# A two-layer transformer kernel: block inputs also sent in by feature, bfloat16 transposes by DMA, biases folded into weights

## The chip, the cores and the metric

The kernel runs on one core of a Trainium2 chip. A core has a matrix engine (TensorE, PE in the profile, with its weight loads as PEld), a vector engine (VectorE, DVE), a scalar engine (ScalarE, ACT), a general engine (GpSimd, POOL) and a queue engine (SyncE, SP). SBUF is the on-chip memory with 128 partitions; matmuls write to PSUM. DMAs are issued from the queues of SP, ACT and POOL. The metric is the device time of the program in microseconds; here it is the median over runs, 1665.76 us.

## The reference: what is computed

The input x has 2 sequences of 2048 tokens with 512 features; a context has 2 x 128 tokens with 512 features. Two layers, each with cross attention and a feed-forward part, are added to x one after the other:

```python
x = x + _L0_xattn_ref(_layernorm(x), ctx, ctx, mask_pad, Wq, Wk, Wv, Wo, ln_g, ln_b)
x = x + _L0_ffn_ref(_layernorm(x), clip_x, clip_down, w_gate, w_up, w_down)
x = x + _L1_xattn_ref(_layernorm(x), ctx, ctx, mask, Wq, bq, Wk, bk, Wv, bv, Wo, bo)
x = x + _L1_ffn_ref(_layernorm(x), Wg, bg, We, be)
```

- Layer 0's attention: a second layer norm with gain and offset (`ln_g`, `ln_b`) on x and on the context, 16 heads of 64 with rotary positions, scores through `30 * tanh(s / 30)`, causal mask and padding mask, softmax, values, output projection.
- Layer 0's feed-forward part: 512 to 1408 and back, `silu(gate) * up`, where activations and weights are rounded to 8-bit steps (weights with a step for each row, activations with one step for the whole tensor).
- Layer 1's attention: 16 heads of 32, biases on all projections, masked scores set to 1e-9, softmax over all 128 keys.
- Layer 1's feed-forward part: a gate of 512 classes; the class with the largest probability, modulo 8, picks one of 8 experts:

```python
probs = softmax(x @ Wg + bg)
idx = argmax(probs)
h = relu(x @ We[e] + be[e])      # e = idx % 8
out = h * probs[idx]
```

## The kernel before

x stays in SBUF as 32 tiles of 128 tokens x 512 features (`xs`, inside `xw`). Matmuls contract over partitions, so whatever is multiplied by a weight must be turned first, with features on the partitions. The kernel turns tiles on TensorE against an identity matrix and copies the result from PSUM to SBUF.

**Layer 0's attention** goes over 16 blocks of 256 tokens (`blocks`, two tiles each), four head groups to a block: 64 units `u`, where `k, g = divmod(u, 4)`. In a unit, `scores(u)`, `queries(u + 2, 0)`, `mixed(u - 1)`, `queries(u + 2, 1)` and `projected(u - 2, t)` follow each other. Before a block can be queried it is normed: `normed(k)` (statistics of each tile, the power -1/2 on POOL), `centered(k)` (subtract the mean, multiply by rstd, on DVE), `turned(k, c0)` (four TensorE transposes, then ACT applies gain and offset on the way from PSUM to `xnT`). `normed` and `centered` of block k + 2 run in the unit g = 2 of block k; `turned(k + 1, ...)` in the units g = 0 and 1.

Between these units the weights of layer 0's feed-forward part are made: at g = 0 and g = 3 one of 26 tiles is quantised (`quantised`, to bfloat16 `wb`) on DVE and the next is loaded; one unit later its `turn()` transposes it on TensorE into `wgT`, `wuT` (4 transposes a tile, 22 tiles) or `wdT` (11 transposes a tile, 4 tiles).

In this stage the order of the instructions of PE, DVE and ACT is the order of the code (`manual_schedule`). POOL's and SP's order is made by the framework's planner, by the time at which it reckons each instruction ready. Every queue runs in its order: an instruction that waits holds those behind it.

**Start.** Wk, the first x tiles, Wv, Wq, more x tiles and Wo are loaded in this order on SP's queue; the weights of keys and values lie in the places of the last 23 x tiles (`homes`), whose loads follow when these are used up. The context is normed, `keys(g)` computed, and in between block 0 is normed; then come values, the first queries, and block 1.

**Layer 0's feed-forward part.** `quantised_x(n)` rounds a tile to int8 and widens it to bfloat16 `xq`; `turned_x(n)` turns it (4 transposes) into `xqT`, a block of 512 tokens. For each of 8 blocks and 11 chunks of 128 hidden features, gate and up are each 4 matmuls; the product `h` goes to DRAM. `turned_x` of the next block's four tiles stands in chunks 3, 5, 7 and 9. In this stage only PE keeps the code's order. Then the down projection reads `h` back.

**Layer 1** goes over the 32 tiles, one iteration `n` each, with several tiles in flight; here PE, DVE, ACT and POOL keep the code's order. POOL adds the output bias (`projected`, L902), makes rstd (L92) and spreads the reciprocal sums (`summed`, L864). `turned2(n)` turns the normed tile, `logits(n)` multiplies it by `wgate`; a first matmul (L927) adds the bias, from `beparts` (the biases in three bfloat16 parts) picked by `sel`. `gated(n)` finds the expert. The finished tile is written to `x_dram`. `we`, the expert weights, are loaded in iteration 0. Tokens are then sorted by expert, and `expert(j)` gathers 128 tokens of one expert, turns them (`turned_x2`), adds the bias (L1120) and multiplies by the expert's weights (L1122): 39 times, two of them within the loop and the rest in the tail.

Of the kernel before, what the change touches and what calls it, by code (L numbers as in the profile page):

```python
# [13 lines left out]
I32 = mybir.dt.int32  # L14
# [29 lines left out]
NJB = NT - NJA + NE - 1  # L44
NOWHERE = float(2**20)
# [13 lines left out]
def two_layers(ctx: ExitStack, tc: tile.TileContext, a, out):  # L59
# [15 lines left out]
    nc.vector.memset(minus_half, -0.5)  # L75

# [65 lines left out]
    with ExitStack() as l0:  # L142
# [41 lines left out]
        for n in order[:NB0]:  # L184
            load(xs[n], x_in[n])
        for c in range(ND):
            wv.append([])
            for f in range(E0 // D):
                w = xs[homes[8 + 2 * c + f]]
                load(w, a["L0_xattn_Wv"][c * P : (c + 1) * P, f * D : (f + 1) * D])  # L190
                wv[c].append(w)
# [13 lines left out]
        tables_in(0)  # L205
        load(wo, a["L0_xattn_Wo"].rearrange("(c p) f -> p c f", p=P))
# [66 lines left out]
        def gate_up_in(name, i):  # L273
            w = wtmp.tile([P, D], F32, name="w_in", tag="w_in")
            load(w, a[name][i * P : (i + 1) * P, :])
            return w

        def gate_up(w, dst, scales, i):
            wb = quantised(w, scales[:, i : i + 1])

            def turn():
                pt = psm.tile([P, ND, P], BF16, name="ptb", tag="m")
                for c in range(ND):
                    nc.tensor.transpose(pt[:, c, :], wb[:, c * P : (c + 1) * P], identb)
                nc.scalar.copy(dst[:, :, i * P : (i + 1) * P], pt)

            return turn
# [6 lines left out]
        def down(w, j):  # L294
            wb = quantised(w, sd[:, j : j + 1])

            def turn():
                for i in range(0, NI, 4):
                    n = min(4, NI - i)
                    pt = psm.tile([P, 4, P], BF16, name="ptb", tag="m")  # L300
                    for c in range(n):
                        nc.tensor.transpose(pt[:, c, :], wb[:, (i + c) * P : (i + c + 1) * P], identb)
                    nc.scalar.copy(wdT[:, i : i + n, j * P : (j + 1) * P], pt[:, :n, :])

            return turn
# [9 lines left out]
        norms, xns, xnTs, ropes, qs, prs, atts, pws = {}, {}, {}, {}, {}, {}, {}, {}  # L315
# [3 lines left out]
        def normed(k):  # L319


            for t, n in enumerate(tiles[k]):
                mv = variance(xs[n])
                ve = small.tile([P, 1], F32, name="ve")
                nc.vector.tensor_scalar(ve, mv[:, 1:2], 1.0 + EPS, EPS * EPS, ALU.mult, ALU.add)
                rr = small.tile([P, 1], F32, name="rr")
                nc.gpsimd.tensor_tensor(rr, ve, minus_half, ALU.pow)
                norms[k, t] = mv, rr

        def centered(k):  # L330
            xns[k] = []
            for t, n in enumerate(tiles[k]):
                mv, rr = norms[k, t]
                xn = mid.tile([P, D], F32, name="xn")
                center(xn, xs[n], mv[:, 0:1], rr)
                xns[k].append(xn)

        def turned(k, c0):

            if c0 == 0:  # L340
                xnTs[k] = mid.tile([P, ND, B0], F32, name="xnT")
            pt = psm.tile([P, 2, B0], F32, name="pt", tag="m")
            for c in range(2):
                for t, xn in enumerate(xns[k]):
                    nc.tensor.transpose(pt[:, c, t * P : (t + 1) * P], xn[:, (c0 + c) * P : (c0 + c + 1) * P], ident)  # L345
            for c in range(2):
                nc.scalar.activation(  # L347
                    xnTs[k][:, c0 + c, :], pt[:, c, :], AF.Identity,
                    bias=lnb[:, c0 + c : c0 + c + 1], scale=lng[:, c0 + c : c0 + c + 1],
# [106 lines left out]
        with tc.manual_schedule(engines={E.PE, E.DVE, E.Activation}):  # L456
            context()
            for g in range(NG):
# [3 lines left out]
                if g == 2:  # L462
                    centered(0)
            nc.vector.tensor_scalar(pad, padu, -1e30, None, ALU.mult)
            for c in range(0, ND, 2):
                turned(0, c)
# [12 lines left out]
            for u in range(nu + 2):  # L479
# [11 lines left out]
                if u > 1:  # L491
                    for t in range(0 if u + 2 < nu or u >= nu else 1, NB0):
                        projected(u - 2, t)
                if g < 2 and k + 1 < nblk:
                    turned(k + 1, 2 * g)
# [8 lines left out]
                if g == 2:  # L504
                    if k > 0:
                        largest(k - 1, 1)
                    if k + 2 < nblk:
                        normed(k + 2)
                        centered(k + 2)
# [38 lines left out]
    beparts = w1.tile([P, D], BF16, name="beparts")  # L548
    sel = w1.tile([P, NE + 1, P], BF16, name="sel")
# [50 lines left out]
    with ExitStack() as up:  # L600
# [6 lines left out]
        cxs = [kv.tile([P, D], F32, name=f"cx{b}") for b in range(B)]  # L607
# [3 lines left out]
        for b in range(B):  # L611
            nc.scalar.dma_start(out=cxs[b], in_=a["ctx_1024"][b])
# [10 lines left out]
        for b in range(B):  # L623
            pt = transposed(psm, cxs[b])
            nc.scalar.copy(ctxT[:, :, b * T : (b + 1) * T], pt)
# [42 lines left out]
        def turned_x(n):  # L668
            blk, t = divmod(n, NBF)
            if t == 0:  # L670
                xqTs[blk] = work.tile([P, ND, BF], BF16, name="xqT", bufs=2)
            pt = psm.tile([P, ND, P], BF16, name="ptx", tag="m")
# [8 lines left out]

        nc.vector.memset(beparts, 0.0)
        nc.vector.memset(ones1, 1.0)
        nc.vector.tensor_scalar(bq, bq, 1.0 / math.sqrt(DH1), None, ALU.mult)
        bparts = kv.tile([NE + 1, 3, D], BF16, name="bparts")
        brest = kv.tile([NE + 1, D], F32, name="brest")
        load(brest[:NE, :], a["L1_ffn_be"])
        load(brest[NE:, :], a["L1_ffn_bg"].rearrange("(o d) -> o d", o=1))
        for k in range(3):
            nc.vector.tensor_copy(bparts[:, k, :], brest)  # L690
            nc.vector.tensor_tensor(brest, brest, bparts[:, k, :], ALU.subtract)
        be_dram = dram.tile([3, NE + 1, D], BF16, name="be_dram")
        nc.sync.dma_start(out=be_dram.rearrange("k e d -> e k d"), in_=bparts)
        for k in range(3):
            load(beparts[16 * k : 16 * k + NE + 1, :], be_dram[k])
        rowi = kv.tile([P, 1], I32, name="rowi")
        nc.gpsimd.iota(rowi, pattern=[[0, 1]], base=0, channel_multiplier=1)
        nc.vector.tensor_scalar(rowi, rowi, 15, None, ALU.bitwise_and)
        rowf = kv.tile([P, 1], F32, name="rowf")
        nc.vector.tensor_copy(rowf, rowi)  # L700
        ei_ = kv.tile([P, NE + 1], I32, name="ei_")
        nc.gpsimd.iota(ei_, pattern=[[1, NE + 1]], base=0, channel_multiplier=0)
        nc.vector.tensor_scalar(sel, ei_.unsqueeze(2).to_broadcast([P, NE + 1, P]), rowf, None, ALU.is_equal)
# [215 lines left out]
    def turned2(n):  # L919
        pt = transposed(psm, xn2[n])  # L920
        xn2T[n] = mid.tile([P, ND, P], F32, name="xnT1", bufs=1)
        nc.scalar.copy(xn2T[n], pt)

    def logits(n):

        pl = pls[n] = psm.tile([P, D], F32, name="pl", tag="m")
        nc.tensor.matmul(pl, sel[:, NE, :], beparts, start=True, stop=False)  # L927
        for c in range(ND):
            nc.tensor.matmul(pl, xn2T[n][:, c, :], wgate[:, c, :], start=False, stop=(c == ND - 1))  # L929
# [176 lines left out]
    def turned_x2(j):  # L1106
        if j < NJ:
            pt = transposed(psm, part(6 + j % 3, [D]))
            ring[j] = part(9 + j % 3, [ND, P])
            nc.scalar.copy(ring[j], pt)  # L1110

    def expert(j):
# [6 lines left out]

        nc.tensor.matmul(pz, sel[:, bass.ds(e, 1), :], beparts, start=True, stop=False)  # L1120
        for c in range(ND):
            nc.tensor.matmul(pz, ring[j][:, c, :], we[:, bass.ds(e, 1), c, :], start=False, stop=(c == ND - 1))  # L1122
# [40 lines left out]
    for n in range(NT):  # L1163
# [29 lines left out]
        if n == 0:  # L1193
# [6 lines left out]
            for e in range(NE):  # L1200
                load(we[:, e], a["L1_ffn_We"][e].rearrange("(c p) f -> p c f", p=P))
        if not ahead:
# [78 lines left out]
```

## Time and profile before

| | |
|---|---|
| median of 3 runs | 1665.76 us (1664.41 to 1665.9) |
| time of the profiled execution | 1666.03 us |
| its span, first to last instruction | 1664.3 us |
| mean granted TensorE clock | 0.998 of full speed |

Busy time by stage (us, from the span's start; counts left out):

| stage | window | PE | DVE | ACT | POOL | DMA share |
|---|---|---|---|---|---|---|
| start | 0 to 62 | 51.60 of 62 | 23.00 | 12.55 | 15.38 | 0.87 |
| layer 0's units | 62 to 275 | 212.59 of 213 | 145.19 | 60.40 | 49.10 | 0.05 |
| layer 0's units | 275 to 560 | 284.02 of 285 | 198.30 | 81.49 | 59.20 | 0.06 |
| layer 0's end | 560 to 690 | 126.43 of 130 | 83.35 | 37.45 | 22.97 | 0.08 |
| to the feed-forward part | 690 to 738 | 44.90 of 48 | 42.69 | 18.89 | 2.46 | 0.52 |
| gate, up, down | 738 to 930 | 189.22 of 192 | 153.17 | 99.41 | 36.93 | 0.62 |
| layer 1's tiles | 1060 to 1450 | 388.45 of 390 | 338.55 | 249.16 | 77.05 | 0.06 |
| experts, tail | 1515 to 1664 | 137.55 of 149 | 50.70 | 38.94 | 67.09 | 0.32 |

A timeline line gives the start, the duration, the engine, the line of the code, the operation, output<-input, shapes, and how many like instructions are merged (x8). A group line gives busy time and the mean of one. Matmuls are pipelined, so the durations of neighbours overlap and a group's mean is longer than the step from one to the next. A DMA issue line ends with the time from the issue to the landing, where the trace shows it.

### The profile page before, as it was taken

The numbers are of one execution on the slowest core, as the hardware profiler recorded it, in microseconds if no ns is written. First come the engines' busy times: TensorE is split into PE (matmuls) and PEld (weight loads), VectorE is DVE, ScalarE is ACT, GpSimd is POOL, SyncE is SP. The second block draws the span as 40 slices with busy tenths as digits, with TensorE's granted clock in tenths as the row PEclk, the third lists the DMA queues.
The fourth block names the chain that finished last, engine by engine and source line by source line (L and its number), as shares of the span: only waits on it lengthen the run. The fifth ranks groups of instructions, "written<-read, shape, count | busy, mean of one in ns | idle before, by whom it ended". The sixth has DMA issues, their size and how long they took to land. (4 is left out here: it accounts for less than half of the span.)

```text
span 1664.3 us, 27098 instructions
## 1 busy us (share of the span) xinstructions
PE 1625.2 (98%) x10277; PEld 977.3 (59%) x10277; DVE 1176.4 (71%) x2294; ACT 709.4 (43%) x1601; POOL 390.8 (23%) x464
## 2 busy tenths in 40 slices
PE   7999999999999999999999999999999999999997
PEld 5666666666666555544444566676767666654553
DVE  3466667776667765699976678888888889875222
ACT  1223222222233222255445576666666666652222
POOL 2322222222222221100006632121211111224453
PEclk9999999999999999999999999999999999999999
DMA  9300000000000000455458750000000000113331
GB/s 331 132 15 18 20 14 20 14 20 14 20 14 8 35 18 1 141 146 158 146 155 282 248 202 15 20 21 14 20 14 20 14 21 14 46 46 103 124 118 62
DMA packets 89454, 118.24 MB, mean 71 GB/s; under 512 B 10732, under 2 KB 58146, under 8 KB 89325
## 3 DMA queue, kind: packets, MB, share of 16 engines
q1 hardware_dynamic: 80076, 96.63, 17.3%
q0 software_dynamic: 6240, 18.70, 3.5%
q8 instruction: 82, 1.34, 0.3%
q10 hardware_dynamic: 3008, 1.19, 0.3%
q14 instruction: 48, 0.39, 0.1%
HBM read 76.55 MB, written 41.77 MB: 71 GB/s over the span
## 5 line engine op out<-in xcount | busy, mean ns | idle before, releaser
L362 PE MATMUL pq<-xnT,wq 128*128 128x256 f32 x1024 | 254.4, 391 | 0.0
L420 PE MATMUL pw<-wo,att 128*128 128x512 f32 x512 | 230.8, 593 | 0.0
L362 PEld LDWEIGHTS pq<-xnT,wq 128*128 128x128 f32 x1024 | 184.4, 189 | 67.1 <-issue 38.7
L855 ACT ACTIVATE s<-s,mx 128x128 f32<-128x128 f32 x512 | 176.7, 387 | 18.0 <-DVE mx L846 18.0
L388 ACT ACTIVATE pr<-sc 128x1024 f32<-128x1024 f32 x64 | 65.9, 1030 | 237.0 <-PE sc L383 236.2
L420 PEld LDWEIGHTS pw<-wo,att 128*128 128x128 f32 x512 | 96.9, 190 | 96.4 <-issue 89.9
L410 DVE RECIPROCAL rd<-sc 128x256 f32<-128x256 f32 x64 | 112.5, 1758 | 51.3 <-PE sc L404 51.3
L372 POOL TENSOR_TENSOR q<-rt,rt 128x256 f32<-128x256 f32 x64 | 46.5, 727 | 422.4 <-DVE rt L371 422.4
L1122 PE MATMUL pz<-we,x 128*128 x312 | 140.3, 592 | 0.0
L367 DVE TENSOR_TENSOR rt<-pq,rope_cos 128x256 f32<-128x256 f32 x64 | 27.2, 425 | 141.2 <-PE pq L362 139.9
L347 ACT ACTIVATE xnT<-pt,lnb,lng 128x256 f32<-128x256 f32 x64 | 32.7, 561 | 216.2 <-PE pt L345 216.2
L813 PE MATMUL pq<-xT,wq 128*128 128x256 f32 x512 | 124.1, 385 | 0.0
L905 PE MATMUL pw<-wo,oT 128*128 128x512 f32 x256 | 115.5, 594 | 1.6 <-DVE oT L897 1.6
L929 PE MATMUL pl<-wgate,xnT 128*128 128x512 f32 x256 | 115.1, 592 | 0.0
L813 PEld LDWEIGHTS pq<-xT,wq 128*128 128x128 f32 x512 | 94.8, 190 | 28.1 <-issue 13.6
L1126 DVE TENSOR_TENSOR x<-x,x 128x512 f32<-128x512 f32 x39 | 27.0, 693 | 97.3 <-ACT x L1125 97.3
L841 DVE SCALAR_TENSOR_TENSOR s<-sc,keep 128x1024 f32<-128x1024 f32 x64 | 78.0, 1219 | 23.8 <-PE sc L833 23.8
L83 DVE BATCH_NORM_STATS2 st<-x 128x6 f32<-128x512 f32 x130 | 89.6, 689 | 6.0 <-DMA x<-in_ctx 3.7
L1122 PEld LDWEIGHTS pz<-we,x 128*128 128x128 f32 x312 | 58.9, 190 | 58.5 <-issue 56.8
L711 PE MATMUL pg<-xqT,wgT 128*128 128x512 bf16 x352 | 90.3, 379 | 0.7 <-ACT xqT L675 0.7
L711 PE MATMUL pu<-xqT,wuT 128*128 128x512 bf16 x352 | 90.3, 379 | 0.0
L716 ACT ACTIVATE gate<-pg,gsc 128x512 f32<-128x512 f32 x88 | 60.5, 687 | 68.9 <-PE pg L711 67.9
(229 smaller groups left out, 2888.9 us busy)
## 6 DMA issues: line engine op xcount, KB each, us to landing
h_dram<-h SPq DMA_DIRECT2D x88, 256.0 KB, 2.1
hq<-h_dram SPq DMA_DIRECT2D x31, 704.0 KB, 5.8
x_dram<-x SPq DMA_DIRECT2D x32, 258.0 KB, 3.0
x<-in_x SPq DMA_DIRECT2D x32, 256.0 KB, 5.7
we<-in_L_ffn_We SPq DMA_DIRECT2D x8, 1024.0 KB, 11.7
w_in<-in_L_ffn_w_gate SPq DMA_DIRECT2D x11, 256.0 KB, 2.6
w_down<-in_L_ffn_w_down SPq DMA_DIRECT2D x4, 704.0 KB, 4.1
w_in<-in_L_ffn_w_up SPq DMA_DIRECT2D x11, 256.0 KB, 2.6
```

Of the source, the lines that this page charges most:

```text
L83: nc.vector.bn_stats(out=st, in_=x)
L362: nc.tensor.matmul(pq, wqs[c // 2][:, c % 2, par, g * P : (g + 1) * P], xnTs[k][:, c, :], start=(c == 0), stop=(c == ND - 1))
L388: nc.scalar.activation(pr, sc[:, :, :B0], AF.Tanh, scale=1.0 / (math.sqrt(DH0) * GROK))
L410: nc.vector.reciprocal(rd, sc[:, 0, B0:])
L420: nc.tensor.matmul(pw, atts[u][:, f, t * P : (t + 1) * P], wo[:, 2 * g + f, :], start=(g == 0 and f == 0), stop=(g == NG - 1 and f == 1),)
L711: nc.tensor.matmul(dst, w[:, c, i * P : (i + 1) * P], xqTs[blk][:, c, :], start=(c == 0), stop=(c == ND - 1),)
L813: nc.tensor.matmul(pq, wq1[:, c, f * P : (f + 1) * P], xTs[blk][:, c, :], start=(c == 0), stop=(c == ND - 1))
L841: nc.vector.scalar_tensor_tensor(s, sc[:, 2 * half : 2 * half + 2].rearrange("p r c k -> p (r c) k"), -MASKED, keeps[n].unsqueeze(1).to_br ...
L855: nc.scalar.activation(s[:, h, :], s[:, h, :], AF.Exp, bias=mx[:, h : h + 1], **accum)
L905: nc.tensor.matmul(pw, os_[n][:, c, :], wo1[:, c, :], start=(c == 0), stop=(c == ND - 1))
L929: nc.tensor.matmul(pl, xn2T[n][:, c, :], wgate[:, c, :], start=False, stop=(c == ND - 1))
L1122: nc.tensor.matmul(pz, ring[j][:, c, :], we[:, bass.ds(e, 1), c, :], start=False, stop=(c == ND - 1))
```

## The change

1. The host also sends x turned by blocks (`x_turned`) and the context turned (`ctx_turned`). Layer 0's blocks load their features directly (`features_in`, three buffers). `normed` gathers mean and rstd of a block in one small tile; `turned_in` writes it to DRAM by token and reads it back broadcast to all partitions (`along`). `centered` subtracts the mean along the tokens on POOL, `scaled` multiplies by rstd on DVE, `affine` applies gain and offset on ACT in place. The TensorE transposes of block inputs are gone. Block 0's two small DMAs go on ACT's queue, the others on SP's.
2. The bfloat16 transposes (gate, up and down weights; rounded x of all blocks but the first) are DMAs with transposition on SP's queue. The buffer for a loaded gate or up tile is one instead of two.
3. Layer 1's context is loaded turned; its eight transposes and two copies are gone.
4. Biases of gate and experts go into the weights. On the way from PSUM, `raised` adds 4 to the features in partition 0 (features 0, 128, 256, 384). A row `v = b / 16 - (sum of those four weight rows) / 4` is added to every row of the weight: a normed token sums to zero over its features, so the raised token times v gives 16 v, and with 4 times the four weight rows the result is b. The rows are made on DVE from small loads, kept in `v_dram`, and added on POOL: 4 additions for `wgate`, then 32 for `we`, two in each of the iterations n = 4 to 19. The bias matmuls are gone, with `beparts` and `sel`.

```diff
+        def features_in(k):
+            xnTs[k] = mid.tile([P, ND, B0], F32, name="xnT", bufs=3)
+            load(xnTs[k], a["x_turned"][k // B, k % B])
...
-            w = wtmp.tile([P, D], F32, name="w_in", tag="w_in")
+            w = wtmp.tile([P, D], F32, name="w_in", tag="w_in", bufs=1)
...
-                pt = psm.tile([P, ND, P], BF16, name="ptb", tag="m")
-                for c in range(ND):
-                    nc.tensor.transpose(pt[:, c, :], wb[:, c * P : (c + 1) * P], identb)
-                nc.scalar.copy(dst[:, :, i * P : (i + 1) * P], pt)
+                nc.sync.dma_start(out=dst[:, :, i * P : (i + 1) * P], in_=wb, transpose=True)
...
+                nc.sync.dma_start(out=wdT[:, :, j * P : (j + 1) * P], in_=wb, transpose=True)
...
         def normed(k):
+            stats[k] = small.tile([P, NB0, 2], F32, name="stat")
             for t, n in enumerate(tiles[k]):
                 mv = variance(xs[n])
                 ve = small.tile([P, 1], F32, name="ve")
                 nc.vector.tensor_scalar(ve, mv[:, 1:2], 1.0 + EPS, EPS * EPS, ALU.mult, ALU.add)
+                nc.vector.tensor_copy(stats[k][:, t, 0:1], mv[:, 0:1])
+                nc.gpsimd.tensor_tensor(stats[k][:, t, 1:2], ve, minus_half, ALU.pow)
+            if k > 1:
+                features_in(k)
+            turned_in(k)
+        def turned_in(k):
+            queue = nc.scalar if k == 0 else nc.sync
+            queue.dma_start(out=stat_dram[k].rearrange("t s p -> p (t s)"), in_=stats.pop(k).rearrange("p t s -> p (t s)"))
+            along[k] = mid.tile([P, NB0, 2, P], F32, name="along", bufs=1)
+            queue.dma_start(out=along[k], in_=stat_dram[k].partition_broadcast(P))
+        def by_token(k, i, op, engine):
+            x = xnTs[k].rearrange("p c (t q) -> p c t q", t=NB0)
+            engine.tensor_tensor(x, x, along[k][:, :, i].unsqueeze(1).to_broadcast([P, ND, NB0, P]), op)
         def centered(k):
+            by_token(k, 0, ALU.subtract, nc.gpsimd)
+        def scaled(k):
+            by_token(k, 1, ALU.mult, nc.vector)
+        def affine(k, c0):
+            for c in range(c0, c0 + 2):
                 nc.scalar.activation(
+                    xnTs[k][:, c, :], xnTs[k][:, c, :], AF.Identity, bias=lnb[:, c : c + 1], scale=lng[:, c : c + 1]
                 )
...
+                if g == 0 and k + 1 < nblk:
+                    scaled(k + 1)
                 if g < 2 and k + 1 < nblk:
-                    turned(k + 1, 2 * g)
+                    affine(k + 1, 2 * g)
...
                     if k + 2 < nblk:
                         normed(k + 2)
-                        centered(k + 2)
+                if g == 3 and k + 2 < nblk:
+                    centered(k + 2)
...
+        nc.scalar.dma_start(out=ctxT, in_=a["ctx_turned"])
...
+            if blk > 0:
+                nc.sync.dma_start(out=xqTs[blk][:, :, t * P : (t + 1) * P], in_=xqs[n], transpose=True)
+                return
...
+        nc.vector.tensor_scalar(vrow, vrow, 1.0 / (ND * RAISE), None, ALU.mult)
+        nc.vector.scalar_tensor_tensor(vrow, wrow[:, 0, :], -1.0 / ND, vrow, ALU.mult, ALU.add)
+        v_dram = dram.tile([NE + 1, D], F32, name="v_dram")
+        nc.sync.dma_start(out=v_dram.rearrange("e (q f) -> (e q) f", f=P), in_=vrow)
+        load(rowadd, v_dram[NE].partition_broadcast(P))
+        for c in range(ND):
+            nc.gpsimd.tensor_tensor(wgate[:, c, :], wgate[:, c, :], rowadd, ALU.add)
...
-        nc.scalar.copy(xn2T[n], pt)
+        nc.scalar.activation(xn2T[n], pt, AF.Identity, bias=raised)
...
-        nc.tensor.matmul(pl, sel[:, NE, :], beparts, start=True, stop=False)
...
-        nc.tensor.matmul(pz, sel[:, bass.ds(e, 1), :], beparts, start=True, stop=False)
...
+        if 4 <= n < 4 + 2 * NE:
+            e, half = divmod(n - 4, 2)
+            if half == 0:
+                load(rowadd, v_dram[e].partition_broadcast(P))
+            for c in range(2 * half, 2 * half + 2):
+                nc.gpsimd.tensor_tensor(we[:, e, c, :], we[:, e, c, :], rowadd, ALU.add)
...
+    arrays["x_turned"] = arrays["x"].reshape(B, S // B0, B0, ND, P).transpose(1, 0, 4, 3, 2)
+    arrays["ctx_turned"] = arrays["ctx_1024"].reshape(B * T, ND, P).transpose(2, 1, 0)
```

## The prediction

> **What bounds the kernel now.** I read the busy shares first, then the groups of instructions by shape, then the timeline of one stretch of each stage, and last the DMA issues.
>
> ```profile
> span 1664.3 us, 27098 instructions
> PE 1625.2 (98%) x10277; PEld 977.3 (59%) x10277; DVE 1176.4 (71%) x2294; ACT 709.4 (43%) x1601; POOL 390.8 (23%) x464
> PE   7999999999999999999999999999999999999997
> ```
>
> PE is busy in every slice but the first and last, so an instruction taken from PE shortens its stage, as long as nothing else becomes late. What it shortens is not its own duration (matmuls overlap) but the step between instruction starts. So I take costs from starts in the timeline. Layer 0's units begin with `L383`:
>
> ```profile
> 285.27 0.71 PE L383 MATMUL sc<-q,kTe 32*128 32x256 f32 x8
> 295.72 0.71 PE L383 MATMUL sc<-q,kTe 32*128 32x256 f32 x8
> ...
> 306.17 0.71 PE L383 MATMUL sc<-q,kTe 32*128 32x256 f32 x8
> 315.96 0.71 PE L383 MATMUL sc<-q,kTe 32*128 32x256 f32 x8
> ...
> 614.17 0.71 PE L383 MATMUL sc<-q,kTe 32*128 32x256 f32 x8
> 626.32 0.71 PE L383 MATMUL sc<-q,kTe 32*128 32x256 f32 x8
> 636.54 0.71 PE L383 MATMUL sc<-q,kTe 32*128 32x256 f32 x8
> ```
>
> A unit with no transposes takes 9.79 us (306.17 to 315.96). One with four of x takes 10.22 (626.32 to 636.54), one with four of x and four of a gate or up weight 10.45 (285.27 to 295.72), one with four of x and eleven of the down weight 12.15 (614.17 to 626.32). So four of x cost 0.43, four of a weight 0.23, eleven 1.93.
>
> The time of the profiled execution is 1666.0 us, 1.7 around its span; it stands 0.3 above the median of the runs, 1665.76.
>
> **What is removed from PE.** Layer 0's loop: 15 blocks x 2 x 0.43 = 12.9, 22 weight tiles x 0.23 = 5.1, 4 down tiles x 1.93 = 7.7, together 25.7 us.
>
> Gate and up stage: the starts are 740.33, 742.28 and 744.00 for three first halves, the first pair with a transposed tile between; 1.95 - 1.72 = 0.23, 28 tiles, 6.4 us. DVE is close behind there (18.34 of 20 us busy in the window 780 to 800), so I take 6; the lower end is 0, if DVE becomes the bound.
>
> The bias matmuls:
>
> ```profile
> 1161.87 0.38 PE L927 MATMUL pl<-beparts,sel 128*128 128x512 bf16 x1
> 1162.09 3.60 PE L929 MATMUL pl<-wgate,xnT 128*128 128x512 f32 x8
> ...
> 1495.57 0.38 PE L1120 MATMUL pz<-beparts,sel 128*128 128x512 bf16 x1
> 1495.79 3.60 PE L1122 MATMUL pz<-we,x 128*128 x8
> ```
>
> They hold PE 0.22 each: 32 gates give 7.0 us, 39 experts up to 8.6. In the expert tail PE idles 11.5 of 149 us, so I take 8. Layer 1's eight context transposes are 1.04 us, and the copy behind them takes about as long: 0 to 2.2, I take 1.5, as the first step of the feed-forward also hangs on DVE. (The turned context, 512 KB on ACT's queue in place of two loads that went out at 690.1 for a use at 698.6, has the same 8.5 us.) Sum removed: 25.7 + 6 + 7 + 8 + 1.5 = 48.2 us.
>
> **What is added off PE.** Per block in layer 0: SP issues a 512 KB load of features, a write of the means and rstd to DRAM in 512 elements of 4 bytes, and, waiting for it, a 256 KB broadcast read; POOL subtracts over 128x1024, DVE multiplies, ACT scales in place as before. DVE loses two centerings (0.54 each) and gains one 128x1024 pass (nearest row `L846`, 1.22) and two copies (0.15): nothing, on an engine with a third of each unit idle. POOL: twice the 1.28 of `L902`, 2.6 us.
>
> Is the chain in time? In the block traced, the last pow ends at 318.4. Legs under load, from rows of the same sizes:
>
> ```profile
> bq<-in_L_xattn_bq SPq DMA_DIRECT2D x1, 2.0 KB, 6.4
> x<-in_x SPq DMA_DIRECT2D x32, 256.0 KB, 5.7
> ```
>
> 318.4 + 6.4 + 5.7 + 2.6 = 333.1. In a quiet queue (3.0 for the `x_dram` store, 2.6 for a `w_in` load) it is 326.6. DVE reaches the multiply after the rope products of that unit, 7.8 us after its start at 325.75: 333.5. Behind the multiply on DVE is the next unit's `L367` (338.7); ACT's scaling is ahead of that unit's tanh (336.7), which PE waits for. With 1.2 for the multiply and 1.0 for the scaling the multiply may start as late as 334.5. So cost 0, with 1.4 to 7.9 us in hand, or the two legs may sum to 13.5 against 5.6 to 12.1. While POOL waits for the broadcast, the rope subtractions (`L372`) queue behind it; they have 4 us before DVE reuses their inputs. SP's waits hold only weight loads with a unit or more in hand, even with one `w_in` buffer.
>
> The start has no such cover. Block 0: pow ends 25.6; legs 5.9 (`bk`, on ACT's queue) and 5.7 give 37.2, POOL 39.8, DVE 41.0, four ACT scalings (0.51 each) 43.1. Queries now start at 37.2: +6. (ACT waits in its own queue for pow and for the write; behind that stand only the scalings and the copies of v, which PE needs later.) Block 1's legs run on SP's queue behind the 23 late x loads (DMA is 0.9 busy there): pow ends 6 us later than the old 42.5, the broadcast lands near 61 (6.4 and 5.7 again), POOL is done near 63 to 66, and DVE meets the multiply near 61.5, 6 us behind the transposes it replaces: +3. Together +9; bounds -2 (the old transposes and their copies hold PE from 28.1 to 30.3; all else hidden) and +25 (two legs of 9.1 like `masks`, +12.5 in either chain).
>
> **Transposes by DMA** are not in this trace. They are hidden if they land in time: the weight tiles are first read after 705; in the gate and up stage the last of four tiles is quantised at 764 and read at the next block, about 770.5. Nearest rows, 2.1 us (`h_dram` store) to 5.7: cost 0; each us beyond 6.5 would cost 7 blocks x 1 us. The Trainium skill speaks against this move ("VectorE: DVE Perf Modes", section on the three transpose paths, and its rules for kernel authors): it gives a 128x128 bf16 transpose 390 ns on TensorE and 1309 ns by DMA, and prefers TensorE where PSUM will do. An estimate from that page is 5.2 us for four, still under the cover, so the sum by it would be the same. TensorE's price here is the 0.23 us above.
>
> **The expert weights** get 32 POOL additions (128x512, 1.28 us) in tiles 4 to 19 of layer 1. POOL has the time; DVE may not:
>
> ```profile
> 1152.45 1.27 POOL L902 TENSOR_TENSOR x<-x,bob 128x512 f32<-128x512 f32 x1
> 1152.55 1.19 DVE L951 TENSOR_TENSOR cum<-cum,hot 128x8 bf16<-128x8 bf16 x1
> ...
> 1483.61 0.16 DVE L951 TENSOR_TENSOR cum<-cum,hot 128x8 bf16<-128x8 bf16 x1
> ```
>
> An 8-element DVE instruction takes 1.19 while POOL adds and 0.16 otherwise: it is held until POOL ends. Two additions right there, behind `L864`, hold DVE up to 2.6 us more. DVE is busy 13.7 of 16 us per tile: 16.3 against PE's 15.7 is 0.6 x 16 = 9 us at most if only the load counts; 0 if other instructions fall there. I take 4. Queued behind the additions on POOL is `L902`, whose sum is read 8 us later: covered. The loads of the added row have a tile's time. The four `wgate` additions fall where POOL idles.
>
> **Sum:** -48.2 + 9 + 4 = -35.2; 1666.0 - 35.2 - 0.3 = 1630 us.
>
> **Rivals.**
> 1. *The statistics come late in every block* (slower). Place: DVE's multiply and ACT's scaling behind it in layer 0. It decides when the two legs pass 13.5 us; each us over costs 14 us, so 2.5 over (16 us) eats the whole gain. With both legs like `masks` (18.2), 4.7 x 14 = 66: 1696 us. For it: 512 tiny packets, and an SP queue that waits between the legs. Against: the DMA share is 0.05 in that stage, so rows measured under load are pessimistic. 0.16.
> 2. *POOL holds DVE in layer 1 and DVE's delay lands on PE* (projection after `L897`): 16 x 2.6 = 41 instead of 4, 1667 us. For it: the 1.19. Against: `L897` has 3 us before PE needs it, and scores have 2. 0.08.
> 3. *DMA transposes land late* in the gate and up stage: 5 us x 7 = 35, 1665 us. 0.06.  For it: DVE runs close there, and stores fill the DMA to 0.5. Against: landings of 2 to 6 us in the same queue.
>
> **How the numbers follow.** Main case 0.70, 1630, its own range 1613 (no cost added, all terms full: 1666 - 49.9 - 2, less 0.3) to 1659 (startup +25, POOL +9, gate stage and context 0). To leave no more than two in ten out, the range goes to 1680, over rivals 2 and 3 and the first us of rival 1. A change under 0.2%, about 3 us, cannot be told from none. Faster: 0.70, 0.03 of rival 1 (legs between 13.5 and 16) and 0.02 of the others; same: 0.05 of rivals 2 and 3, whose price is about the gain; slower: 0.13 of rival 1 and 0.07 where 2 or 3 meets a dear start: 0.75, 0.05, 0.20.
>
> **What would show it.** Layer 0's units all near 9.8 us, with no `L345`, `L284`, `L302`; a PE gap of 5 to 15 us between 35 and 65 us; broadcast reads landing within 12 us of the pow; gate and up steps all 1.72; layer 1 tiles near 15.7, those of n = 4 to 19 slightly longer with `cum` at 1.2 and centerings stretched. Wrong if DVE waits for POOL at the multiply each block, if PE waits for a transposed tile, or if the start costs more than 25 us.

## The result

The changed kernel takes 1721.4 us (median of 4 runs, 1721.18 to 1723.5), the kernel before 1665.22 in the same comparison (4 runs): ratio 1.034, 95% interval 1.0323 to 1.0358. It is slower by 56 us, where 35 us less was forecast. The profiled execution of the changed kernel has a span of 1719.5 us and a mean granted clock of 0.978 (before: 1664.3 and 0.998).

First the page of the changed kernel: its span, busy times, and the slices for PE and its granted clock.

```profile
span 1719.5 us, 26387 instructions
PE 1607.8 (94%) x9826; PEld 949.9 (55%) x9826; DVE 1194.2 (69%) x2306; ACT 684.3 (40%) x1537; POOL 487.1 (28%) x514
PE   5699999999999999998999999999999999999997
PEclk9899999999999999999999999999999999999999
```

PE's instructions went from 10277 to 9826, but its busy time only from 1625.2 to 1607.8 us, and its share from 98% to 94%: it waits, and part of what is left runs slower. The waits of the changed kernel (engine, line, releaser: us in total, times, longest):

```profile
DVE rt L382 <- POOL q L387: 138.2, 15, 10.5
PE sc L398 <- DVE att L426: 42.4, 15, 4.3
PE pq L377 <- ACT xnT L363: 15.3, 1, 15.3
POOL xnT L353 <- issue: 124.6, 9, 14.6
POOL xnT L353 <- DMA along<-stat_dram: 95.0, 7, 15.8
```

Fifteen times, about once a block, DVE's rope products wait for POOL and PE waits for DVE; one long wait of PE stands at the start. POOL itself waits in its subtraction along the tokens (`L353`), sixteen times, for the broadcast (nine of these the profile names only as "issue").

From the starts of PE's score matmuls (`L383` before, `L398` after) each run is cut into three terms: to the fifth unit (the second block's first), from there to the last unit of layer 0, and the rest of the span. All runs of this study, in us:

| kernel | to the fifth unit | fifth to last unit | rest |
|---|---|---|---|
| before | 83.09 | 600.31 | 980.90 |
| changed | 104.36 | 646.45 | 968.69 |
| e1, old block input | 81.45 | 587.75 | 968.90 |
| e2, subtraction on DVE | 103.19 | 580.88 | 971.53 |
| e3, POOL in written order | 106.81 | 583.34 | 969.45 |
| e4, statistics written in one piece | 91.04 | 575.52 | 968.54 |
| e5, statistics a unit earlier | 107.36 | 692.95 | 968.39 |
| e6, as e5, two blocks by rows | 81.39 | 693.22 | 969.19 |
| e7, two sets of rope products | 109.11 | 604.35 | 967.64 |
| e8, only transposes by DMA | 82.01 | 587.74 | 975.45 |
| e9, as e6, POOL in written order | 81.55 | 575.52 | 968.23 |
| e10, as e5, POOL in written order | 109.22 | 575.52 | 969.56 |

So the change lost 21.3 us at the start and 46.1 in layer 0's loop, and gained 12.2 behind it. The timeline of one block of the changed kernel shows the loss (start, us, engine, line, operation; in brackets the idle time before and its releaser):

```profile
317.03 0.71 PE L398 MATMUL sc<-q,kTe 32*128 32x256 f32 x8
318.73 0.56 POOL L338 TENSOR_TENSOR stat<-ve,minus_half 128x1 f32<-128x1 f32 x1 [0.52 <-DVE stat L337]
319.31 0.38 SPq L347 DMA_DIRECT2D stat_dram<-stat  x1
326.82 0.71 PE L398 MATMUL sc<-q,kTe 32*128 32x256 f32 x8
327.56 0.33 SPq L349 DMA_DIRECT2D along<-stat_dram  x1
332.92 2.34 POOL L353 TENSOR_TENSOR xnT<-xnT,along 128x1024 f32<-128x1024 f32 x1 [13.64 <-issue]
335.22 0.73 POOL L387 TENSOR_TENSOR q<-rt,rt 128x256 f32<-128x256 f32 x1
335.99 0.42 DVE L382 TENSOR_TENSOR rt<-pq,rope_cos 128x256 f32<-128x256 f32 x1 [9.21 <-POOL q L387]
337.01 1.75 DVE L425 RECIPROCAL rd<-sc 128x256 f32<-128x256 f32 x1
339.63 0.71 PE L398 MATMUL sc<-q,kTe 32*128 32x256 f32 x8 [2.94 <-DVE att L426]
340.06 1.70 DVE L353 TENSOR_TENSOR xnT<-xnT,along 128x1024 f32<-128x1024 f32 x1
341.79 1.09 ACT L363 ACTIVATE xnT<-xnT,lnb,lng 128x256 f32<-128x256 f32 x2 [11.55 <-DVE xnT L353]
343.85 0.64 PE L419 MATMUL sc<-pr,ones 128*32 128x256 f32 x8 [1.15 <-ACT pr L403]
```

The unit at 317.03 lasts 9.79 us as forecast, the one at 326.82 lasts 12.81. The write of the statistics is issued at 319.31 and its end lets the read go at 327.56 (8.25 us); the read lands by 332.92 (5.4). POOL has stood in `L353` since 319.3. Behind it in POOL's queue is the rope subtraction `L387` of the unit begun at 317.03, due 7.5 us after that unit's start, at about 324.5; it runs at 335.22. DVE's next rope product (`L382`) needs the buffers that it reads: it comes at 335.99, 6 us behind its place of about 330, and holds the reciprocal and the weighted sums behind it on DVE, for which PE waits. The loss goes on into the next unit, which lasts 11.01 us: DVE's multiply is now late too, ACT's scaling behind it stands ahead of the tanh (`L403`), and PE waits 1.15 us for that. Over the loop the changed kernel is 70.9 us above e4 below, whose loop has no such wait: 47.6 of them are in units like that at 326.82, 23.3 in the units behind.

### The profile page after: what moved, and what is told of

It is laid out like the page before. It is cut to its first block, busy times and chain, and to the rows that moved or that the text cites. A ratio compares the mean times of both kernels' runs of the same rounds, so it can differ in the third digit from the quotient of the medians.

```text
span 1719.5 us, 26387 instructions
## 1 busy us (share of the span) xinstructions
PE 1607.8 (94%) x9826; PEld 949.9 (55%) x9826; DVE 1194.2 (69%) x2306; ACT 684.3 (40%) x1537; POOL 487.1 (28%) x514
## 5 line engine op out<-in xcount | busy, mean ns | idle before, releaser
L377 PE MATMUL pq<-xnT,wq 128*128 128x256 f32 x1024 | 269.2, 409 | 15.3 <-ACT xnT L363 15.3
L377 PEld LDWEIGHTS pq<-xnT,wq 128*128 128x128 f32 x1024 | 194.2, 200 | 89.2 <-issue 47.3
L403 ACT ACTIVATE pr<-sc 128x1024 f32<-128x1024 f32 x64 | 65.2, 1019 | 329.7 <-PE sc L398 230.8
L870 ACT ACTIVATE s<-s,mx 128x128 f32<-128x128 f32 x512 | 176.7, 387 | 18.2 <-DVE mx L861 18.1
L382 DVE TENSOR_TENSOR rt<-pq,rope_cos 128x256 f32<-128x256 f32 x64 | 27.0, 422 | 196.1 <-POOL q L387 138.2
L363 ACT ACTIVATE xnT<-xnT,lnb,lng 128x256 f32<-128x256 f32 x64 | 34.6, 589 | 211.6 <-DVE xnT L353 200.5
L387 POOL TENSOR_TENSOR q<-rt,rt 128x256 f32<-128x256 f32 x64 | 46.5, 726 | 235.8 <-DVE rt L386 235.8
L828 PEld LDWEIGHTS pq<-xT,wq 128*128 128x128 f32 x512 | 94.8, 190 | 28.1 <-issue 13.6
L353 POOL TENSOR_TENSOR xnT<-xnT,along 128x1024 f32<-128x1024 f32 x16 | 37.5, 2342 | 219.6 <-issue 124.6
L398 PE MATMUL sc<-q,kTe 32*128 32x256 f32 x512 | 49.4, 456 | 48.7 <-DVE att L426 42.4
L100 POOL TENSOR_TENSOR x<-ve,minus_half 128x1 f32<-128x1 f32 x32 | 17.6, 550 | 263.7 <-DVE ve L99 263.7
```

Of the source, the lines that this page charges most:

```text
L377: nc.tensor.matmul(pq, wqs[c // 2][:, c % 2, par, g * P : (g + 1) * P], xnTs[k][:, c, :], start=(c == 0), stop=(c == ND - 1))
L403: nc.scalar.activation(pr, sc[:, :, :B0], AF.Tanh, scale=1.0 / (math.sqrt(DH0) * GROK))
L828: nc.tensor.matmul(pq, wq1[:, c, f * P : (f + 1) * P], xTs[blk][:, c, :], start=(c == 0), stop=(c == ND - 1))
L870: nc.scalar.activation(s[:, h, :], s[:, h, :], AF.Exp, bias=mx[:, h : h + 1], **accum)
```

## The experiments

What was to be told apart (these numbers are the experiments' own, not those of the prediction's rivals): **theory 1**, the order on POOL, as just read; **rival 2**, the statistics are too late for the multiply and ACT's scaling, whatever POOL's order; **rival 3**, the lower granted clock costs by itself; **rival 4**, the transposes by DMA hold SP's queue or PE; **rival 5**, the write in 4-byte pieces is the term. Unless said otherwise each is one execution, beside one of the kernel before (1664.6 to 1666).

**e1: the old block input.** Part 1 of the change is undone, so `normed`, `centered` and `turned` are those of before.

```diff
-                if g == 0 and k + 1 < nblk:
-                    scaled(k + 1)
                 if g < 2 and k + 1 < nblk:
-                    affine(k + 1, 2 * g)
+                    turned(k + 1, 2 * g)
```

> The changed kernel with the block input of the kernel before (norm on rows, 16 float32 transposes on PE, evictions on ACT); the rest of the change stays: bfloat16 transposes by DMA, the turned context, the biases in the weights. Theory 1 (the loss is all in the new block input): the start and layer 0's units are those of before less the weight transposes (5.1 + 7.7 us of PE, so 640 to about 627 from first to last unit), and with the 1.9, 1.8 and 8.1 us already seen behind layer 0 the time is 1640 (1633 to 1648). Rival 4 (the DMA transposes and their places on SP's queue hold layer 0): units stay above 660 and the time above 1675. If the lower granted clock came from the DMA transposes, it shows 0.96 in layer 0 here too; if from PE's stalls, about 1.00.

Measured 1640.1, granted clock 0.998. The whole loss is in the new block input; rival 4 falls, and the clock does not come from the transposes by DMA.

**e2: the subtraction on DVE.**

```diff
-            by_token(k, 0, ALU.subtract, nc.gpsimd)
...
+            by_token(k, 0, ALU.subtract, nc.vector)
             by_token(k, 1, ALU.mult, nc.vector)
```

> The changed kernel with the subtraction of the means moved from POOL to DVE, directly ahead of the multiply, in every block: nothing on POOL waits for the broadcast any more, and DVE gets a second operation of about 1.7 us in each block's first unit. Theory 1 (POOL's queue: the subtraction waits for the broadcast and holds the rope subtractions of the unit behind it, about 5.4 us in each of 14 to 15 blocks): the waits of DVE's rope products on POOL (138 us) go, the unit with g = 3 is back near 10 us, and what is left is a tanh later by the second DVE operation, 1 to 3 us a block: 1655 to 1680. Rival 2 (the turned statistics are simply too late for the scaling, whatever the order on POOL): DVE waits for the broadcast instead, the block stays near 46 us, 1705 to 1725.

Measured 1657.5. The loop falls from 646.45 to 580.88; what PE still waits for in the loop is the tanh (4.4 us in 14 times; one more wait of 6.0 stands in the start). Rival 2 falls as the main cause: the write takes as long as before (8.5 to 11.8 us in the loop), and late data and the second DVE pass together cost 5.4 us over e4's loop.

**e3: POOL in written order.** With POOL in the manual schedule, `L353` follows the rope subtractions of its unit; the order on the other engines and queues stays.

```diff
-        with tc.manual_schedule(engines={E.PE, E.DVE, E.Activation}):
+        with tc.manual_schedule(engines={E.PE, E.DVE, E.Activation, E.Pool}):
```

> The changed kernel with POOL's instructions kept in the order in which they are written, in layer 0: the subtraction now stands behind the rope subtractions of its unit; PE, DVE, ACT and SP keep their order to the instruction. Theory 1: the rope subtractions no longer wait (5.4 us a block comes back), but the data are as late as before (subtraction done 335.2 where DVE's multiply would come at about 333.5), so 1.5 to 4 us of each block stay, on the path through the multiply, ACT's scaling and the tanh: 1670 to 1695. Rival 2 (data late, order without effect): 1710 to 1725. If the loss is POOL's order alone: 1640 to 1655.

Measured 1662.2, better than theory 1 expected (1670 to 1695); the start stays long (106.81). The same stretch of a block in this run's timeline:

```profile
307.54 0.33 SPq L349 DMA_DIRECT2D along<-stat_dram  x1
312.99 2.35 POOL L353 TENSOR_TENSOR xnT<-xnT,along 128x1024 f32<-128x1024 f32 x1 [7.80 <-issue]
315.30 0.73 POOL L387 TENSOR_TENSOR q<-rt,rt 128x256 f32<-128x256 f32 x1
315.37 1.73 DVE L353 TENSOR_TENSOR xnT<-xnT,along 128x1024 f32<-128x1024 f32 x1 [1.62 <-POOL xnT L353]
315.76 0.71 PE L398 MATMUL sc<-q,kTe 32*128 32x256 f32 x8
```

The broadcast lands as late as before, in the next unit; the multiply waits 1.62 us for POOL, and PE feels it only through the tanh (6.8 us in 8 times within the loop). The order on POOL is worth 646.45 - 583.34 = 63.1 us, the lateness at the multiply 583.34 - 575.52 = 7.8 (both over 14 blocks).

**e4: the statistics written in one piece.** The tokens get other tokens' statistics; all else is the same work.

```diff
-            queue.dma_start(out=stat_dram[k].rearrange("t s p -> p (t s)"), in_=stats.pop(k).rearrange("p t s -> p (t s)"))
+            queue.dma_start(out=stat_dram[k].rearrange("t s p -> (t s p)").rearrange("(p i) -> p i", p=P), in_=stats.pop(k).rearrange("p t s -> p (t s)"))
```

> The changed kernel with the statistics written to DRAM in one piece of 16 bytes for each partition in place of four of 4 bytes that lie apart; order and number of all other instructions stay. The layout is not turned, so each token gets other tokens' statistics; amounts and times are the same. Rival 5 (the size of the write is the term: 8.25 us quiet, 11 to 13 us at the start): the write falls to 2 to 5 us, the broadcast lands 4 to 6 us earlier, POOL holds nobody, start and layer 0 both gain, 1630 to 1655. Theory 1 agrees with this in direction (its wait is order times lateness) and expects 1640 to 1665. If the write's length comes from its completion or from queueing and not from its pieces, the leg stays above 7 us and the time above 1700.

Measured 1637.6; its timeline at the same place:

```profile
318.47 0.33 SPq L347 DMA_DIRECT2D stat_dram<-stat  x1
321.82 0.33 SPq L349 DMA_DIRECT2D along<-stat_dram  x1
324.98 2.35 POOL L353 TENSOR_TENSOR xnT<-xnT,along 128x1024 f32<-128x1024 f32 x1 [6.54 <-DVE inv L283]
```

The write takes 3.35 us here in place of 8.25, and with it both losses go: all units of the loop but its last three (10.01, 10.01 and 7.26 in every run) are 9.79, and the start is 8 us behind that of before in place of 21. The time lies in the range of rival 5 (1630 to 1655) and 2 below that of theory 1, so this run alone does not part the two. In the loop order and lateness are both needed: taking away the lateness gives back all of the 70.9 us, taking away the order 63.1.

**e5 and e6: the statistics one unit earlier.** e6 also norms the first two blocks on rows, with the old transposes.

```diff
+                if g == (1 if k else 2) and k + 2 < nblk:
+                    normed(k + 2)
+                if g == 2 and k > 0:
+                    for t in range(NB0):
+                        largest(k - 1, t)
...
-                    affine(k + 1, 2 * g)
+                    (affine if k > 0 else turned)(k + 1, 2 * g)
```

> The changed kernel with the statistics of block k+2 made, written and fetched one unit earlier (in the unit with g = 1; one of the two searches for the largest value goes to g = 2 in exchange), from the second block on. The write stays in pieces of 4 bytes, POOL's subtraction stays where it is. Theory 1 (an order on POOL that costs only because the broadcast is late): with some 10 us more of lead the broadcast lands ahead of the subtraction, every unit from block 1 on is 9.79 as in the run with the short write (575.5 us from the second block's first unit to the last), the start stays as in the changed kernel (second block at about 104 us): 1648 to 1658. Rival 5 in its narrow form (the many small pieces cost by themselves, by the load that they put on the DMA engines): the units stay above 10 on the mean, time above 1670.

> The kernel with the earlier statistics, and the first two blocks normed on rows and transposed on PE as in the kernel before, so that no statistic is needed while the first loads run. Theory 1 with the start as a term of its own: second block's first unit at 81.5 us as in the run with the old block input, then 575.5 us to the last unit and 968.5 behind it, 1627.5 (1622 to 1635), faster than both kernels and than the old block input alone (1640). If the token-wise path has a cost in steady state that the short write took away (the load of the small pieces, DVE's 1.7 us multiply ahead of ACT's scaling), it is 1636 or more.

Measured 1770.7 and 1746.0 (e6: ratio 1.0482, interval 1.0465 to 1.05). Both expectations of theory 1 failed: more lead made it worse. By the number alone both runs lie where rival 5 was put (above 1670, and 1636 or more). The timeline of e5 shows another reason:

```profile
328.74 0.38 SPq L347 DMA_DIRECT2D stat_dram<-stat  x1
337.76 0.33 SPq L349 DMA_DIRECT2D along<-stat_dram  x1
342.96 2.34 POOL L353 TENSOR_TENSOR xnT<-xnT,along 128x1024 f32<-128x1024 f32 x1 [14.25 <-issue]
346.02 0.42 DVE L382 TENSOR_TENSOR rt<-pq,rope_cos 128x256 f32<-128x256 f32 x1 [11.61 <-POOL q L387]
349.66 1.24 PE L398 MATMUL sc<-q,kTe 32*128 32x256 f32 x8 [6.06 <-DVE att L426]
```

The subtraction moved with the statistics: it stands directly behind the last pow, which ended at 328.71, where the 14.25 us of idle time begin, and ahead of rope subtractions due 3 us later. That the code has it in the unit with g = 3 has no effect: POOL is left to the planner. And part of the lead goes on DVE, which does `finished` first: the pow ends 4.8 us behind its unit's start (323.95), in the changed kernel 2.3, so DVE's next product waits longer.

**e7: two sets of rope products** (and two buffers of turned features, for room); the order on PE, DVE, ACT and POOL is that of the changed kernel, that on SP's queue is not.

```diff
-                ropes[u] = [mid.tile([P, B0], F32, name=f"rt{i}", bufs=1) for i in range(4)]
+                ropes[u] = [mid.tile([P, B0], F32, name=f"rt{i}", bufs=2) for i in range(4)]
```

> The changed kernel with two sets of rope products in place of one (room made by two buffers of the turned features in place of three); the order on PE, DVE, ACT and POOL stays to the instruction, the subtraction still stands ahead of its unit's rope subtractions on POOL and waits for the broadcast. Theory 1: the wait on POOL reaches DVE and PE only through the single buffers, since the rope's results are wanted two units later; DVE's 138 us of waits on POOL go, the time falls to that of POOL in hand-written order, 1655 to 1675. If POOL's order costs by another way (late queries for the scores, or late scaled features), the time stays above 1695. If two buffers of the features are too few, the wait shows on the load of the features in the sync queue.

Measured 1682.9, 8 us above the range. DVE's waits on POOL's rope are gone and 42.1 of the 70.9 us above 575.52 come back, so the single buffers did pass most of the wait on. Not all: the score matmuls now wait for the late queries themselves (4.2 and 12.0 us behind `L387` and `L389` within the loop), which theory 1 had put out of reach, as the rope's results are wanted two units later.

**e8: only the transposes by DMA**, on the kernel before.

```diff
-                    nc.tensor.transpose(pt[:, c, :], wb[:, c * P : (c + 1) * P], identb)
-                nc.scalar.copy(dst[:, :, i * P : (i + 1) * P], pt)
+                nc.sync.dma_start(out=dst[:, :, i * P : (i + 1) * P], in_=wb, transpose=True)
```

> The kernel before with nothing but the bfloat16 transposes by DMA (gate, up and down weights in layer 0, the quantised rows in the gate/up stage). By the sum of the prediction: 5.1 + 7.7 us in layer 0 and 6.4 in the gate/up stage, 1645.5; by the stage table of the changed kernel the gate/up stage gives only 2 to 3: 1649 to 1651. The biases in the weights and the turned context then hold what is left of the 24.5 us that the run with the old block input gained, about 10. If the DMA transposes held something, above 1655.

Measured 1647.1. The loop gives 12.6 us (587.74), and from the first gate matmul to the first of the down projection the stage takes 160.74 against 166.66 before: 5.9. So nearly the full gain of the gate and up stage (6.4 in the sum) is there when the transposes come alone.

**e9 and e10: e6 and e5 with POOL in written order**, the one line of e3.

> The slow run with rows for the first two blocks and earlier statistics (1746), with POOL in written order in layer 0 and nothing else: PE, DVE, ACT and SP stay to the instruction, the subtraction moves from ahead of the rope subtractions of an earlier unit to behind those of the unit with g = 3, when the broadcast should have landed. Theory 1 as it now stands (the planner, left free, puts the subtraction on POOL a fixed distance behind the statistics, so that earlier statistics only move the wait earlier): all units from block 1 on are 9.79, second block's first unit at 81.5, 575.5 from there, 968.5 behind: 1627.5 (1622 to 1635), faster than both kernels. If the small writes or the scaling's place on DVE and ACT cost something by themselves, units over 9.9 and 1636 to 1660.

> The run with earlier statistics (1771) with POOL in written order in layer 0 and nothing else; the start is that of the changed kernel, statistics for blocks 0 and 1 through DRAM under the first loads. Theory 1: units 9.79 from the second block on, which begins at 104 to 107: 1648 to 1656, so that the start alone is some 23 to 26 us against the run above. If the start's loss is made good later, below 1645; if steady units still wait, above 1665.

Measured 1629.0 (e9: median of 4, 1627.18 to 1629.8; ratio to the kernel before 0.978, interval 0.9763 to 0.9796) and 1656.4. The timeline of e9 (its lines are shifted: `L345` is the write, `L347` the read, `L420` the first rope subtraction, `L386` the subtraction and the multiply, `L431` the scores):

```profile
301.72 0.38 SPq L345 DMA_DIRECT2D stat_dram<-stat  x1
310.85 0.33 SPq L347 DMA_DIRECT2D along<-stat_dram  x1
314.32 0.72 POOL L420 TENSOR_TENSOR q<-rt,rt 128x256 f32<-128x256 f32 x1 [8.08 <-DVE rt L419]
315.94 2.35 POOL L386 TENSOR_TENSOR xnT<-xnT,along 128x1024 f32<-128x1024 f32 x1 [0.22 <-DMA along<-stat_dram]
316.51 0.71 PE L431 MATMUL sc<-q,kTe 32*128 32x256 f32 x8
324.21 1.70 DVE L386 TENSOR_TENSOR xnT<-xnT,along 128x1024 f32<-128x1024 f32 x1
326.30 0.71 PE L431 MATMUL sc<-q,kTe 32*128 32x256 f32 x8
```

The write is even longer here (9.1 us), the broadcast lands at 315.9, and nobody feels it: the multiply comes 6 us after POOL is done. PE, DVE, ACT and SP have the order of e6, so that one line of POOL's schedule is worth 117 us there. Rival 5 in its narrow form falls with it: the same small pieces are written, and the loop is that of e4. e10 is 0.4 above its range; against e9 it gives the price of the start: 27.7 us to the fifth unit.

## Why the prediction was wrong, step by step

**The step that failed** is the one that costed the steady chain at nothing. It said: "While POOL waits for the broadcast, the rope subtractions (`L372`) queue behind it; they have 4 us before DVE reuses their inputs." The queue and the releaser were right, the comparison was not made. These two lines of the kernel before stand in the block that it costed:

```profile
323.55 0.73 POOL L372 TENSOR_TENSOR q<-rt,rt 128x256 f32<-128x256 f32 x1 [5.19 <-DVE rt L371]
328.92 0.43 DVE L367 TENSOR_TENSOR rt<-pq,rope_cos 128x256 f32<-128x256 f32 x1 [3.21 <-PE pq L362]
```

The forecast's own chain had POOL blocked from the pow at 318.4 to 333.1; the rope subtraction due at 323.55 falls in the middle of that, and 4 us of cover do not hold out 9.6. The chain was measured only against DVE's multiply, at 333.5. For the rope product at 328.92 the broadcast would have had to land at about 325.6 (less POOL's 2.6 and 0.7), so the two legs had 7.2 us, where the forecast allowed 13.5 and itself put 12.1. Measured were 13.6 in the block shown. By e3 the wrong order is worth 63 us, and by e4 and e9 nothing else in the loop is missing. The forecast does not say where in POOL's order the subtraction would stand: in the order as written (e3) it stands behind the rope subtractions of its unit, and the planner put it ahead of them.

**Rival 1** had the right sign for the wrong first consumer. It let the statistics decide past 13.5 us at the multiply; the legs took 13.2 to 14.9 us in the loop, and by e3 that mechanism alone is worth 7.8 us. The late multiply and tanh of the changed kernel (the 23.3 us) are its place, but not its reason: the multiply at 340.06 starts 4.8 us after POOL is done, held by DVE's late rope products. Its price at 18.2 (1696) would not have reached the result either.

**The removals in layer 0** were right: 9.79 for each unit that has no wait, and 600.31 to 575.52 without the waits, 24.8 where 25.7 was summed from the first block on. Transposes by DMA cost nothing there (e8).

**The start** was priced at +9, with +25 as the bound, and came to +21.3. For block 0 the place was right and the legs too short; its chain in the changed kernel was

```profile
23.61 0.39 ACTq L347 DMA_DIRECT2D stat_dram<-stat  x1
36.54 0.34 ACTq L349 DMA_DIRECT2D along<-stat_dram  x1
43.69 2.34 POOL L353 TENSOR_TENSOR xnT<-xnT,along 128x1024 f32<-128x1024 f32 x1 [15.76 <-DMA along<-stat_dram]
46.06 1.73 DVE L353 TENSOR_TENSOR xnT<-xnT,along 128x1024 f32<-128x1024 f32 x1 [18.27 <-POOL xnT L353]
48.48 3.39 PE L377 MATMUL pq<-xnT,wq 128*128 128x256 f32 x8 [15.35 <-ACT xnT L363]
```

a write of 12.9 us and a read of 7.2 in place of 5.9 and 5.7, taken from the rows for `bk` and `x`. The row for `bk` has the same 2.0 KB in the same pieces, but it is a read from DRAM, and this is a write. Of the 21.3 us, 12.8 are there at the first unit. Block 1's broadcast lands at 71.9, where the forecast had 61, and there too the rope subtraction behind it on POOL is what PE feels: the second unit's scores wait 6.3 us for `L387`, where the forecast looked at the multiply. With the one-piece write (e4) the start is +8.0.

**The gate and up stage** was to give 6 and gave 2.7 (166.66 to 163.92). The reserve "DVE becomes the bound" came true only in so far as PE waits for DVE. The two kernels' busy times in this stage, before and then changed (window; its length; PE, PEld, DVE, ACT, POOL; clock; DMA share; GB/s):

```profile
711.60:878.20 166.60, 165.59 (x833) 78.22 (x833) 147.15 (x243) 80.77 (x121) 1.27 (x1) 1.00 0.50 148
```

```profile
778.60:942.50 163.90, 159.30 (x720) 71.55 (x719) 146.85 (x243) 64.01 (x93) 6.59 (x5) 1.00 0.62 177
```

PE has 6.3 us less to do, as summed, but idles 4.6 where it idled 1.0; 3.4 of it is for DVE's `h` products. DVE itself is no busier than before. It waits for buffers of `h`, whose stores go out late:

```profile
791.60 5.32 POOL L718 TENSOR_TENSOR wgate<-wgate,rowadd 128x512 f32<-128x512 f32 x4 [21.47 <-DMA rowadd<-v_dram]
796.95 0.34 SPq L74 DMA_DIRECT2D rowadd<-v_dram  x1
797.38 5.00 SPq L737 DMA_DIRECT2D h_dram<-h  x5
801.24 0.75 DVE L734 SCALAR_TENSOR_TENSOR h<-pu,usc,gate 128x512 f32<-128x512 f32 x1 [1.44 <-DMA h_dram<-h]
```

The load of the next added row waits on SP's queue 5.5 us for POOL's four additions to `wgate`, and five stores of `h` stand behind it: the same kind of hold as on POOL. A second wait of DVE for these stores, 2.1 us at 815.85, has a like in e8 (2.2), which has the same transposes but no such load and loses only 0.5 of the 6.4. That the load is all of the difference was not tried by a run of its own.

**Behind it** the forecast held: 549.71 to 546.67 from layer 1's first score to its last gate (-3.0; the sum had -7 and +4), 146.80 to 139.92 in the expert tail (-6.9; the sum had -8). `cum` still takes 1.19 us while POOL adds, now 2.5 us for two additions. PE loses 0.45 us in every second tile with additions (17.22 from gate to gate in place of 16.77, eight times, 3.6 us): that is the +4 of the sum, and rival 2 of the prediction with its 41 did not come. Nor did its rival 3 (e8).

**The clock** was not in the forecast at all. A view of the changed kernel in stretches around one wait (same columns):

```profile
413.00:423.00 10.00, 10.00 (x66) 5.79 (x64) 0.77 (x2) 2.17 (x2) 2.48 (x2) 1.00 0.23 66
423.00:427.20 4.20, 0.34 (x1) 0.01 (x1) 3.33 (x5) 0.00 (x0) 1.23 (x2) 0.95 0.00 0
427.20:431.00 3.80, 3.78 (x20) 2.78 (x21) 3.66 (x8) 1.61 (x3) 2.39 (x2) 0.50 0.00 0
431.00:434.70 3.70, 3.70 (x30) 1.81 (x29) 1.08 (x3) 2.52 (x4) 0.00 (x0) 0.65 0.88 108
```

After 3.9 us of idle PE the granted clock is 0.50 and comes back some 6 us later. Nine of thirteen blocks looked at this way have such a fall behind the wait, four have none; these four take 43.0 to 43.4 us, the nine 43.3 to 46.1 (means 43.3 and 44.6, against 39.16 without waits). So by this comparison the clock holds at most 1.3 of the 5.4 us that such a block loses, part of that being longer waits, and slower matmuls partly fill time in which PE would wait for the tanh. Rival 3 is real, a minor part, and follows from the waits: e1 and e9 have 0.998.

## What to carry to other kernels

When an instruction that waits for a DMA is added to an in-order engine, the deadline is that of the first instruction queued behind it, not that of its own reader; write down what each of them is due for and take the earliest. An engine whose order a planner sets may put the waiting instruction far ahead of where it is written, so giving its data more lead can make things worse: fix the order (one word here, 1746 to 1629 us) and give the lead with it. A detour through DRAM with a scattering write is cheap only where work covers it: its two legs took 13 to 15 us in the loop; with the multiply 22 us behind the pow (e9) nothing was lost, with about 15 (e3) 7.8 us. At the start of a kernel, keep the path that needs no such round trip (27.7 us between e10 and e9).

## What the runs showed of the hardware

- A write of 2 KB as 512 pieces of 4 bytes took, from its issue to that of the read that waits for it, 8.1 to 11.1 us in the changed kernel's loop (8.25 in the block shown; 8.9 to 11.5 in e9), 12.9 and 11.2 under the first loads. The same 2 KB as 128 pieces of 16 bytes (e4) took 1.4 to 3.5 in the loop, and at the start 6.1 and 1.9.
- Waits of PE before the scores, in the changed kernel's loop: all seven from 2.96 us on (2.96 to 4.26) and those of 2.49 and 2.50 were followed by a fall of the granted clock (0.50 to 0.8 in windows over it), those of 2.51, 2.82, 2.92 and 2.94 by none. The Trainium skill ("TensorE: Matmul & The Clock Gate", "Part 1: The HAM clock gate") has the clock fall to half after an idle window of about 3.4 us in a window that runs freely. The falls here agree in size; gaps a good deal shorter than 3.4 us were enough in some blocks.
- A DVE pass over 128x1024 with one operand repeated over the chunks took 1.70 us and the same on POOL 2.34 (forecast: 1.22 and 2.6). A transposing DMA held SP's queue for 1.19 to 1.29 us in 49 of 54 issues, and up to 3.5 in the others.
